# Attention blocks in f32: key tiles in batches of four and five instead of two, with PSUM shared out anew

## The chip, the cores and the metric

The kernel runs on one core of a Trainium2 chip. The core has an engine for matrix products (TensorE, PE in the profile; its weight loads are PEld), one for vectors (VectorE, DVE), one for functions of single elements (ScalarE, ACT), GpSimd (POOL) and SyncE (SP), which here only issues transfers. They run side by side and wait for one another by semaphores. Matrix products are written to PSUM, which has eight banks of 128 partitions x 512 f32; everything else lies in SBUF. The metric is the device time of one execution, in microseconds (us).

## The reference

The input x has 4 images of 128 channels and 96 x 96 pixels, in f32. Two layers of the same form follow each other, each with its own weights:

```
g     = maxpool2(conv1x1(x, g_w, g_b))          # 64 channels, 48 x 48 = 2304 values
theta = conv1x1(x, theta_w, theta_b)            # 64 channels, 9216 queries
phi   = maxpool2(conv1x1(x, phi_w, phi_b))      # 64 channels, 2304 keys
f     = einsum('bqc,bck->bqk', theta, phi)
y     = einsum('bqk,bkc->bqc', softmax(f, axis=-1), g)
W_y   = conv1x1(y, W_w, W_b)                    # back to 128 channels
out   = batchnorm(W_y; gamma, beta, mean, var) + x
```

So each of the 8 blocks (4 images x 2 layers) is an attention of 9216 queries over 2304 keys with 64 channels, and a residual.

## The kernel before

`shifted_blocks` computes all 8 blocks, image by image, layer 0 and then layer 1. The softmax is taken with a constant shift (35) in place of each query's maximum; two running tiles, `rmax` and `rmin`, keep the extremes of the reciprocal sums, and at the very end a flag tells whether any left the safe range. Only then would `general_blocks`, a second version with true maxima, compute everything anew; in the profiled execution none of its lines appears.

A **block** begins with `keys_and_values`: 24 chunks of x go through one product that gives g and phi together (`gphi_ps`, L156), VectorE pools each chunk by a maximum (L159), ScalarE centres phi and copies it to the other 64 partitions (L173, L176), and g is transposed on TensorE (`gT_ps`, L179) and given its bias (L182).

Then come 9 **pairs**. A pair is 2 x 512 queries, `PT` = 1024. Its two halves lie on partitions 0 to 63 and 64 to 127, so that two small products run on TensorE side by side. An f32 product stands as two matmul instructions in the profile, so that what one tile needs is four instructions. There are two shapes:
- `theta` (L200), `values` (L239) and `denominators` (L247) take 128 rows and 64 columns of the array for each half, 128*64 in the profile;
- `scores` (L221) and `project` (L267) take 64 rows and 128 columns, 64*128.

For each of the 18 key tiles (128 keys, `NKT` = 18), `scores(k)` writes a tile of 128 keys x 1024 queries to PSUM (`sc`, two banks), ScalarE takes the exp into SBUF (`exp`, L226, six buffers) and VectorE adds it to a running sum (L230, L232). `values(k)` adds the product of the exp with g to `av` in PSUM, over all 18 tiles. After that, `denominators` sums `sum` over the partitions by a product with ones (`den`), VectorE takes the reciprocals in four pieces (`rc`, L253), multiplies (`y`, L255), and updates `rmax` and `rmin` (L256, L257). `project` multiplies with the output weights (`W_ps`, two tiles of one bank), and VectorE adds the shift and x (L273), in place of x for layer 0 and into a tile that is sent out for layer 1.

The **order** is written by hand at the end of `block` (L286 to L310): key tiles go in batches of `KB` = 2, so nine batches a pair. Step t issues the scores of batch t, then a `project` that has fallen due, then the values of batch t-1, then a `denominators` that has fallen due. The theta of the next pair is issued in the middle of a pair (j = 4). `denominators` follows one step after a pair's last values, `project` three steps after that. What is left at the end of a block is issued at once. On top of this, the framework puts each engine's instructions in order before the run, by its own estimate of what is ready and with program order as priority; each engine then works through its queue in that order.

**PSUM** has eight banks: `ps_sc` 2 tiles of two banks (scores, and the chunks of gphi), `ps_av` 2 of one, `ps_misc` 2 of one (theta, den, W_ps, the transposes). A tile that is asked for while all places of its kind are in use waits until one is released by its last reader.

Of the kernel before, what the change touches and what calls it, by code (L numbers as in the profile page):

```python
# [9 lines left out]
F32 = mybir.dt.float32  # L10
I32 = mybir.dt.int32
AF = mybir.ActivationFunctionType
ALU = mybir.AluOpType
AX = mybir.AxisListType
PSUM = bass.MemoryType.PSUM

P = 128
B, C, CI, H, W = 4, 128, 64, 96, 96
HW = H * W
NK = (H // 2) * (W // 2)  # L20
QT = 512
NQ = HW // QT
KT = 128
NKT = NK // KT
# [7 lines left out]

PT = 2 * QT
NP = HW // PT
KB = 2
NB = NKT // KB
SHIFT = 35.0
SUM_MIN, SUM_MAX = 1e-20, 1e30

# [2 lines left out]
def shifted_blocks(ctx: ExitStack, tc: tile.TileContext, x: bass.AP, layers, out: bass.AP, flag):  # L42
# [11 lines left out]
    nc = tc.nc  # L54
# [3 lines left out]
    xp = ctx.enter_context(tc.tile_pool(name="xp", bufs=2))  # L58
    kvp = ctx.enter_context(tc.tile_pool(name="kvp", bufs=2))
    work = ctx.enter_context(tc.tile_pool(name="work", bufs=2))  # L60
    ps_sc = ctx.enter_context(tc.tile_pool(name="ps_sc", bufs=2, space=PSUM))
    ps_av = ctx.enter_context(tc.tile_pool(name="ps_av", bufs=2, space=PSUM))
    ps_misc = ctx.enter_context(tc.tile_pool(name="ps_misc", bufs=2, space=PSUM))

    ident = const.tile([P, P], F32, name="ident")
    make_identity(nc, ident)
# [6 lines left out]
    rmax = const.tile([P, QT], F32, name="rmax")  # L73
    nc.gpsimd.memset(rmax, 1.0)
    rmin = const.tile([P, QT], F32, name="rmin")
# [132 lines left out]
    class Pair:  # L208
# [9 lines left out]
        def scores(self, k):  # L218
            ps = ps_sc.tile([P, PT], F32, tag="sc", name=f"sc_{self.name}_{k}")
            for h in range(2):  # L220
                nc.tensor.matmul(  # L221
                    ps[:, ts(h, QT)], lhsT=self.phi[ts(h, CI), ts(k, KT)],
                    rhs=self.th[ts(h, CI), :], start=True, stop=True,
                )
            e = work.tile([P, PT], F32, tag="exp", name=f"exp_{self.name}_{k}", bufs=6)
            nc.scalar.activation(e, ps, AF.Exp, bias=nshift)  # L226
            self.es[k] = e
            if k == 1:
                self.sum = work.tile([P, PT], F32, tag="sum", name=f"sum_{self.name}")
                nc.vector.tensor_add(self.sum, self.es[0], e)  # L230
            elif k > 1:
                nc.vector.tensor_add(self.sum, self.sum, e)  # L232

        def values(self, k):
            if k == 0:
                self.av = ps_av.tile([P, QT], F32, tag="av", name=f"av_{self.name}")
            e = self.es.pop(k)
            for h in range(2):
                nc.tensor.matmul(  # L239
                    self.av[ts(h, CI), :], lhsT=self.gT[:, k, :], rhs=e[:, ts(h, QT)],  # L240
                    start=(k == 0), stop=(k == NKT - 1),
                )

        def denominators(self):
            ps = ps_misc.tile([P, QT], F32, tag="misc", name=f"den_{self.name}")
            for h in range(2):
                nc.tensor.matmul(  # L247
                    ps[ts(h, CI), :], lhsT=ones, rhs=self.sum[:, ts(h, QT)],
                    start=True, stop=True,
                )  # L250
            rc = work.tile([P, QT], F32, tag="rc", name=f"rc_{self.name}")
            for i in range(QT // P):
                nc.vector.reciprocal(rc[:, ts(i, P)], ps[:, ts(i, P)])  # L253
            self.y = work.tile([P, QT], F32, tag="y", name=f"y_{self.name}")
            nc.vector.tensor_mul(self.y, self.av, rc)  # L255
            nc.vector.tensor_tensor(rmax, rmax, rc, ALU.max)  # L256
            nc.vector.tensor_tensor(rmin, rmin, rc, ALU.min)  # L257

        def project(self):
            if self.store is not None:  # L260
                dst = work.tile([C, PT], F32, tag="out", name=f"out_{self.name}")
            else:
                dst = self.xt[:, ts(self.p, PT)]
            pss = []
            for h in range(2):
                ps = ps_misc.tile([P, QT], F32, tag="misc", name=f"W_ps_{self.name}_{h}")
                nc.tensor.matmul(  # L267
                    ps, lhsT=self.w["W"][ts(h, CI), :], rhs=self.y[ts(h, CI), :],
                    start=True, stop=True,
                )  # L270
                pss.append(ps)
            for h in range(2):
                nc.vector.scalar_tensor_tensor(  # L273
                    dst[:, ts(h, QT)], pss[h], self.w["shift"],
                    self.xt[:, ts(2 * self.p + h, QT)], op0=ALU.add, op1=ALU.add,
                )
            if self.store is not None:
                nc.sync.dma_start(out=self.store[:, ts(self.p, PT)], in_=dst)

    def block(xt, w, store, name):  # L280
        phi, gT = keys_and_values(xt, w, name)

        def pair(p):
            return Pair(xt, w, phi, gT, p, store, name)

        hooks = {}  # L286
        batches = [(p, j) for p in range(NP) for j in range(NB)]
        pairs = {0: pair(0)}
        for t in range(len(batches) + 1):
            if t < len(batches):  # L290
                p, j = batches[t]
                for k in range(j * KB, (j + 1) * KB):
                    pairs[p].scores(k)
            for step in hooks.pop((t, "rows"), []):
                step()
            if t:
                p, j = batches[t - 1]
                for k in range(j * KB, (j + 1) * KB):
                    pairs[p].values(k)
                if j == NB // 2 and p + 1 < NP:  # L300
                    pairs[p + 1] = pair(p + 1)
                if j == NB - 1:
                    done = pairs.pop(p)
                    hooks.setdefault((t + 1, "columns"), []).append(done.denominators)
                    hooks.setdefault((t + 4, "rows"), []).append(done.project)
            for step in hooks.pop((t, "columns"), []):
                step()
        for key in sorted(hooks):
            for step in hooks[key]:
                step()  # L310

    xt = load_x(0)
    ws = [load_layer(l, p) for l, p in enumerate(layers)]
    for b in range(B):
        nxt = load_x(b + 1) if b + 1 < B else None
        block(xt, ws[0], None, f"{b}_0")
        block(xt, ws[1], out[b].rearrange("c h w -> c (h w)"), f"{b}_1")
        xt = nxt
# [6 lines left out]
    ps = ps_misc.tile([P, QT], F32, tag="misc", name="bad_ps")  # L325
# [7 lines left out]
def general_blocks(ctx: ExitStack, tc: tile.TileContext, x: bass.AP, layers, out: bass.AP):  # L333
# [9 lines left out]
    nc = tc.nc  # L343
# [5 lines left out]
    kvp = ctx.enter_context(tc.tile_pool(name="kvp", bufs=2))  # L349
    work = ctx.enter_context(tc.tile_pool(name="work", bufs=3))  # L350
    ps_max = ctx.enter_context(tc.tile_pool(name="ps_max", bufs=3, space=PSUM))
    ps_sc = ctx.enter_context(tc.tile_pool(name="ps_sc", bufs=2, space=PSUM))
    ps_av = ctx.enter_context(tc.tile_pool(name="ps_av", bufs=2, space=PSUM))
    ps_misc = ctx.enter_context(tc.tile_pool(name="ps_misc", bufs=1, space=PSUM))

    ident = const.tile([P, P], F32, name="ident")
# [240 lines left out]
def nonlocal_blocks(tc: tile.TileContext, x: bass.AP, layers, out: bass.AP):  # L597
    with tc.tile_pool(name="flag", bufs=1) as pool:
        flag = pool.tile([1, 1], I32, name="flag")
        shifted_blocks(tc, x, layers, out, flag)  # L600
        bad = tc.nc.values_load(flag[0:1, 0:1])
        with tc.If(bad > 0):
            general_blocks(tc, x, layers, out)
# [30 lines left out]
```

## Time and profile before

| | |
|---|---|
| time, median of 3 runs (lowest, highest) | 2915.18 us (2915.01, 2915.45) |
| the profiled execution: time, span of its trace | 2915.95 us, 2913.7 us |
| mean granted clock of TensorE | 0.993 |
| exp on ScalarE (L226) | 1296 x 1110 ns |
| sums on VectorE (L232) | 1152 x 1221 ns |
| reciprocals on VectorE (L253) | 288 x 908 ns |
| a score matmul (L221), a value matmul (L239) | 5184 x 615 ns, 5184 x 605 ns |

The profile is of one execution; a row of a timeline gives start, duration, engine, line, operation, output and inputs with shapes and the number of instructions merged into it, and in brackets how long the engine had been idle and what ended that. Matmuls are pipelined and two run side by side here, so their durations overlap and their ends are modelled: what they cost is read from the distance between starts.

### The profile page before, as it was taken

Reading aid. Unit: us, or ns where it says so; the run is one execution under the profiler, and the core shown is the slowest. Engines: PE = TensorE matmul, PEld = TensorE weight load, DVE = VectorE, ACT = ScalarE, POOL = GpSimd, SP = SyncE. Lnnn points to the kernel's source line nnn. Section 1 sums busy time; section 2 is a strip of 40 time slices with the busy share of each in tenths; the row PEclk is TensorE's granted clock in tenths of the full one; section 3 lists DMA queues with packets and bytes.
Section 4 is the critical chain, followed back from the end, with each engine's and each line's share of the span. In section 5 each row is a group of like instructions: output and inputs, shape, how many; then the busy total and the mean of one; then the engine's idle time right before and its main releaser. Section 6 shows DMA issues by size and latency. Waiting matters only on the chain.

```text
span 2913.7 us, 29776 instructions
## 1 busy us (share of the span) xinstructions
PE 2842.7 (98%) x11768; PEld 913.5 (31%) x11768; DVE 2071.7 (71%) x2131; ACT 1467.4 (50%) x1420; POOL 1.6 (0%) x8
## 2 busy tenths in 40 slices
PE   7999999999999999999999999999999999999998
PEld 2333333333333333333333333333333333333332
DVE  4777767777677776777767777677776777767776
ACT  3555535555355553555545555455544555445554
POOL 0000000000000000000000000000000000000000
PEclk9999999999999999999999999999999999999999
DMA  3000000000100000000010000000000000000000
GB/s 135 1 1 1 1 1 15 15 15 15 73 1 1 1 1 0 15 15 15 15 73 1 1 1 0 1 15 15 15 15 8 1 0 1 1 0 15 15 15 23
DMA packets 11604, 40.06 MB, mean 14 GB/s; under 512 B 3393, under 2 KB 3777, under 8 KB 11457
## 3 DMA queue, kind: packets, MB, share of 16 engines
q1 hardware_dynamic: 8640, 37.75, 3.3%
q8 instruction: 94, 1.54, 0.2%
q10 hardware_dynamic: 2816, 0.34, 0.1%
q14 instruction: 54, 0.43, 0.0%
HBM read 19.21 MB, written 18.87 MB: 13 GB/s over the span
## 4 chain that ended last, share of the span: by engine, by line
PE 95%; DVE 2%; ACT 1%; DMA 1%; issue 0%; ACTq 0%
PE sc L221 42%; PE av L239 41%; PE gphi_ps L156 4%; PE theta_ps L200 2%; PE W_ps L267 2%; PE den L247 2%; DVE rc L253 1%; DVE gphi L159 1%; PE gT_ps L179 1%; DMA theta_b<-in_L_conv_theta_b_dram 0%; ACT exp L226 0%; DVE centre L169 0%; ACT phi L173 0%; DMA W_nat<-in_L_conv_W_w_dram 0%; ACT phi L176 0%; DMA theta_nat<-in_L_conv_theta_w_dram 0%
## 5 line engine op out<-in xcount | busy, mean ns | idle before, releaser
L226 ACT ACTIVATE exp<-sc,nshift 128x1024 f32<-128x1024 f32 x1296 | 1372.5, 1110 | 1083.7 <-PE sc L221 1083.5
L232 DVE TENSOR_TENSOR sum<-sum,exp 128x1024 f32<-128x1024 f32 x1152 | 1406.3, 1221 | 556.6 <-ACT exp L226 492.2
L221 PE MATMUL sc<-theta,phi 64*128 64x512 f32 x5184 | 1289.0, 615 | 12.6 <-ACT exp L226 8.0
L239 PE MATMUL av<-exp,gT 128*64 128x512 f32 x5184 | 1253.5, 605 | 0.0
L221 PEld LDWEIGHTS sc<-theta,phi 64*128 64x128 f32 x5184 | 445.3, 186 | 840.3 <-issue 457.3
L239 PEld LDWEIGHTS av<-exp,gT 128*64 128x64 f32 x5184 | 315.0, 136 | 859.8 <-issue 853.7
L253 DVE RECIPROCAL rc<-den 128x128 f32<-128x128 f32 x288 | 243.7, 908 | 12.8 <-PE den L247 12.8
L230 DVE TENSOR_TENSOR sum<-exp,exp 128x1024 f32<-128x1024 f32 x72 | 88.2, 1225 | 175.7 <-ACT exp L226 175.7
L156 PE MATMUL gphi_ps<-x,gphiT 128*128 128x384 f32 x384 | 170.5, 556 | 35.6 <-DVE gphi L159 30.5
L159 DVE TENSOR_REDUCE gphi<-gphi_ps 128x96 f32<-128x384 f32 x192 | 105.5, 554 | 62.7 <-PE gphi_ps L156 57.5
L205 ACT ACTIVATE theta<-theta_ps,theta_b 128x512 f32<-128x512 f32 x72 | 49.5, 687 | 150.1 <-PE theta_ps L200 150.1
L173 ACT ACTIVATE phi<-gphi,centre 64x768 f32<-64x768 f32 x24 | 22.3, 930 | 172.1 <-DVE centre L170 136.1
L156 PEld LDWEIGHTS gphi_ps<-x,gphiT 128*128 128x128 f32 x384 | 66.4, 202 | 101.3 <-DVE gphi L159 56.3
L200 PE MATMUL theta_ps<-x,thetaT 128*64 128x512 f32 x288 | 84.0, 595 | 0.0
L267 PE MATMUL W_ps<-y,WT 64*128 64x512 f32 x288 | 77.2, 614 | 4.2 <-DVE y L255 4.2
L247 PE MATMUL den<-sum,ones 128*64 128x512 f32 x288 | 74.0, 592 | 0.0
L273 DVE SCALAR_TENSOR_TENSOR x<-W_ps,shift,x 128x512 f32<-128x512 f32 x72 | 53.6, 744 | 2.7 <-PE W_ps L267 2.7
L273 DVE SCALAR_TENSOR_TENSOR out<-W_ps,shift,x 128x512 f32<-128x512 f32 x72 | 53.5, 744 | 0.8 <-PE W_ps L267 0.8
L257 DVE TENSOR_TENSOR rmin<-rmin,rc 128x512 f32<-128x512 f32 x72 | 49.3, 684 | 0.0
L256 DVE TENSOR_TENSOR rmax<-rmax,rc 128x512 f32<-128x512 f32 x72 | 49.0, 681 | 0.0
L255 DVE TENSOR_TENSOR y<-av,rc 128x512 f32<-128x512 f32 x72 | 48.7, 677 | 0.0
L267 PEld LDWEIGHTS W_ps<-y,WT 64*128 64x128 f32 x288 | 27.4, 188 | 39.1 <-issue 15.8
(45 smaller groups left out, 144.2 us busy)
## 6 DMA issues: line engine op xcount, KB each, us to landing
x<-in_x_dram SPq DMA_DIRECT2D x24, 768.0 KB, 7.5
out_dram<-out SPq DMA_DIRECT2D x36, 512.0 KB, 2.6
theta_nat<-in_L_conv_theta_w_dram ACTq DMA_DIRECT2D x2, 32.0 KB, 5.4
theta_b<-in_L_conv_theta_b_dram ACTq DMA_DIRECT2D x4, 0.2 KB, 6.1
gphi_nat<-in_L_conv_g_w_dram ACTq DMA_DIRECT2D x2, 32.0 KB, 5.6
gphi_nat<-in_L_conv_phi_w_dram ACTq DMA_DIRECT2D x2, 32.0 KB, 5.2
g_b<-in_L_conv_g_b_dram ACTq DMA_DIRECT2D x2, 32.0 KB, 5.5
W_nat<-in_L_conv_W_w_dram ACTq DMA_DIRECT2D x2, 32.0 KB, 5.9
```

The lines of the kernel that those rows point to most:

```text
L156: nc.tensor.matmul(ps[:, :CC], lhsT=w["gphi"], rhs=xt[:, ts(r, CC)], start=True, stop=True)
L159: nc.vector.tensor_reduce(gphi[:, ts(r, CC // 4)].rearrange("p (h w) -> p h w", w=W // 2), ps[:, :CC].rearrange("p (h a w b) -> p h w a b" ...
L200: nc.tensor.matmul(ps[ts(h, CI), :], lhsT=w["theta"], rhs=xt[:, ts(2 * p + h, QT)], start=True, stop=True,)
L221: nc.tensor.matmul(ps[:, ts(h, QT)], lhsT=self.phi[ts(h, CI), ts(k, KT)], rhs=self.th[ts(h, CI), :], start=True, stop=True,)
L226: nc.scalar.activation(e, ps, AF.Exp, bias=nshift)
L230: nc.vector.tensor_add(self.sum, self.es[0], e)
L232: nc.vector.tensor_add(self.sum, self.sum, e)
L239: nc.tensor.matmul(self.av[ts(h, CI), :], lhsT=self.gT[:, k, :], rhs=e[:, ts(h, QT)], start=(k == 0), stop=(k == NKT - 1),)
L247: nc.tensor.matmul(ps[ts(h, CI), :], lhsT=ones, rhs=self.sum[:, ts(h, QT)], start=True, stop=True,)
L253: nc.vector.reciprocal(rc[:, ts(i, P)], ps[:, ts(i, P)])
L267: nc.tensor.matmul(ps, lhsT=self.w["W"][ts(h, CI), :], rhs=self.y[ts(h, CI), :], start=True, stop=True,)
L273: nc.vector.scalar_tensor_tensor(dst[:, ts(h, QT)], pss[h], self.w["shift"], self.xt[:, ts(2 * self.p + h, QT)], op0=ALU.add, op1=ALU.add,)
```

## The change

The key tiles of a pair go in four batches of 4, 5, 4 and 5 in place of nine of 2. `ps_sc` gets a third tile (six banks), `ps_av` and `ps_misc` keep one bank each; there are ten exp buffers in place of six.

`denominators` is issued one step earlier, ahead of the pair's last values, and ends with the reciprocals. Behind the last values, ScalarE copies `av` to SBUF, and VectorE multiplies that copy with the reciprocals and updates `rmax` and `rmin`. `project` comes one step later, behind the scores of the next pair's second batch, into one tile of the scores' kind (two banks), and one addition of 128x1024 takes the place of two of 128x512. The next pair's theta is issued behind the values of the second batch. The pools of `general_blocks` are shared out anew as well.

```diff
-KB = 2
-NB = NKT // KB
+BATCHES = ((0, 1, 2, 3), (4, 5, 6, 7, 8), (9, 10, 11, 12), (13, 14, 15, 16, 17))
+NB = len(BATCHES)
...
-    ps_sc = ctx.enter_context(tc.tile_pool(name="ps_sc", bufs=2, space=PSUM))
-    ps_av = ctx.enter_context(tc.tile_pool(name="ps_av", bufs=2, space=PSUM))
-    ps_misc = ctx.enter_context(tc.tile_pool(name="ps_misc", bufs=2, space=PSUM))
+    ps_sc = ctx.enter_context(tc.tile_pool(name="ps_sc", bufs=3, space=PSUM))
+    ps_av = ctx.enter_context(tc.tile_pool(name="ps_av", bufs=1, space=PSUM))
+    ps_misc = ctx.enter_context(tc.tile_pool(name="ps_misc", bufs=1, space=PSUM))
...
-            e = work.tile([P, PT], F32, tag="exp", name=f"exp_{self.name}_{k}", bufs=6)
+            e = work.tile([P, PT], F32, tag="exp", name=f"exp_{self.name}_{k}", bufs=10)
...
+            if k == NKT - 1:
+                self.y = work.tile([P, QT], F32, tag="y", name=f"y_{self.name}")
+                nc.scalar.copy(self.y, self.av)
+                nc.vector.tensor_mul(self.y, self.y, self.rc)
+                nc.vector.tensor_tensor(rmax, rmax, self.rc, ALU.max)
+                nc.vector.tensor_tensor(rmin, rmin, self.rc, ALU.min)
...
-            rc = work.tile([P, QT], F32, tag="rc", name=f"rc_{self.name}")
+            self.rc = rc = work.tile([P, QT], F32, tag="rc", name=f"rc_{self.name}")
             for i in range(QT // P):
                 nc.vector.reciprocal(rc[:, ts(i, P)], ps[:, ts(i, P)])
-            self.y = work.tile([P, QT], F32, tag="y", name=f"y_{self.name}")
-            nc.vector.tensor_mul(self.y, self.av, rc)
-            nc.vector.tensor_tensor(rmax, rmax, rc, ALU.max)
-            nc.vector.tensor_tensor(rmin, rmin, rc, ALU.min)
...
-            pss = []
+            ps = ps_sc.tile([P, PT], F32, tag="sc", name=f"W_ps_{self.name}")
             for h in range(2):
-                ps = ps_misc.tile([P, QT], F32, tag="misc", name=f"W_ps_{self.name}_{h}")
                 nc.tensor.matmul(
-                    ps, lhsT=self.w["W"][ts(h, CI), :], rhs=self.y[ts(h, CI), :],
-                    start=True, stop=True,
-                )
-                pss.append(ps)
-            for h in range(2):
-                nc.vector.scalar_tensor_tensor(
-                    dst[:, ts(h, QT)], pss[h], self.w["shift"],
-                    self.xt[:, ts(2 * self.p + h, QT)], op0=ALU.add, op1=ALU.add,
-                )
+                    ps[:, ts(h, QT)], lhsT=self.w["W"][ts(h, CI), :],
+                    rhs=self.y[ts(h, CI), :], start=True, stop=True,
+                )
+            nc.vector.scalar_tensor_tensor(
+                dst, ps, self.w["shift"], self.xt[:, ts(self.p, PT)],
+                op0=ALU.add, op1=ALU.add,
+            )
...
-        for t in range(len(batches) + 1):
+        ending = None
+        for t in range(len(batches) + 2):
             if t < len(batches):
                 p, j = batches[t]
-                for k in range(j * KB, (j + 1) * KB):
+                for k in BATCHES[j]:
                     pairs[p].scores(k)
-            for step in hooks.pop((t, "rows"), []):
-                step()
-            if t:
+            if ending is not None:
+                ending.project()
+                ending = None
+            if 0 < t <= len(batches):
                 p, j = batches[t - 1]
-                for k in range(j * KB, (j + 1) * KB):
+                if j == NB - 1:
+                    ending = pairs[p]
+                    ending.denominators()
+                for k in BATCHES[j]:
                     pairs[p].values(k)
-                if j == NB // 2 and p + 1 < NP:
+                if j == 1 and p + 1 < NP:
                     pairs[p + 1] = pair(p + 1)
-                if j == NB - 1:
-                    done = pairs.pop(p)
-                    hooks.setdefault((t + 1, "columns"), []).append(done.denominators)
-                    hooks.setdefault((t + 4, "rows"), []).append(done.project)
-            for step in hooks.pop((t, "columns"), []):
-                step()
-        for key in sorted(hooks):
-            for step in hooks[key]:
-                step()
```

More of the change, by code (lines that the diff above doesn't have):

```diff
@@ L284, in pair @@
             return Pair(xt, w, phi, gT, p, store, name)
-        hooks = {}
         batches = [(p, j) for p in range(NP) for j in range(NB)]
         pairs = {0: pair(0)}
-        for t in range(len(batches) + 1):
+        ending = None
+        for t in range(len(batches) + 2):
             if t < len(batches):
                 p, j = batches[t]
-                for k in range(j * KB, (j + 1) * KB):
+                for k in BATCHES[j]:
                     pairs[p].scores(k)
-            for step in hooks.pop((t, "rows"), []):
-                step()
-            if t:
+            if ending is not None:
+                ending.project()
+                ending = None
+            if 0 < t <= len(batches):
                 p, j = batches[t - 1]
-                for k in range(j * KB, (j + 1) * KB):
+                if j == NB - 1:
+                    ending = pairs[p]
+                    ending.denominators()
+                for k in BATCHES[j]:
                     pairs[p].values(k)
-                if j == NB // 2 and p + 1 < NP:
+                if j == 1 and p + 1 < NP:
                     pairs[p + 1] = pair(p + 1)
-                if j == NB - 1:
-                    done = pairs.pop(p)
-                    hooks.setdefault((t + 1, "columns"), []).append(done.denominators)
-                    hooks.setdefault((t + 4, "rows"), []).append(done.project)
-            for step in hooks.pop((t, "columns"), []):
-                step()
-        for key in sorted(hooks):
-            for step in hooks[key]:
-                step()
     xt = load_x(0)
@@ L351, in general_blocks @@
     ps_max = ctx.enter_context(tc.tile_pool(name="ps_max", bufs=3, space=PSUM))
-    ps_sc = ctx.enter_context(tc.tile_pool(name="ps_sc", bufs=2, space=PSUM))
-    ps_av = ctx.enter_context(tc.tile_pool(name="ps_av", bufs=2, space=PSUM))
+    ps_sc = ctx.enter_context(tc.tile_pool(name="ps_sc", bufs=3, space=PSUM))
+    ps_av = ctx.enter_context(tc.tile_pool(name="ps_av", bufs=1, space=PSUM))
     ps_misc = ctx.enter_context(tc.tile_pool(name="ps_misc", bufs=1, space=PSUM))
```

## The prediction

> **What bounds the kernel.** I read the page's busy line first, then the chain, then the timeline of TensorE.
>
> ```profile
> PE 2842.7 (98%) x11768; PEld 913.5 (31%) x11768; DVE 2071.7 (71%) x2131; ACT 1467.4 (50%) x1420; POOL 1.6 (0%) x8
> ...
> PE 95%; DVE 2%; ACT 1%; DMA 1%; issue 0%; ACTq 0%
> ...
> 1026.78:1063.41 36.63, 36.63 (x158) 11.51 (x156) 26.91 (x27) 19.75 (x19) 0.00 (x0) 1.00 0.00 0
> ```
>
> TensorE is busy for 98% and is 95% of the chain. The third line is one pair (1024 queries) from the view by windows: 36.63 us, TensorE busy throughout at granted clock 1.00, VectorE for 26.9, ScalarE for 19.75. So only less time on TensorE makes this faster, and the timeline says what its time goes to (start, duration, line, count):
>
> ```profile
> 1002.35 1.99 PE L221 MATMUL sc<-theta,phi 64*128 64x512 f32 x8
> 1004.17 1.02 PE L267 MATMUL W_ps<-y,WT 64*128 64x512 f32 x4
> 1005.12 1.94 PE L239 MATMUL av<-exp,gT 128*64 128x512 f32 x8
> 1006.99 1.99 PE L221 MATMUL sc<-theta,phi 64*128 64x512 f32 x8
> 1008.91 1.94 PE L239 MATMUL av<-exp,gT 128*64 128x512 f32 x8
> 1010.68 1.03 PE L200 MATMUL theta_ps<-x,thetaT 128*64 128x512 f32 x4
> 1011.63 1.99 PE L221 MATMUL sc<-theta,phi 64*128 64x512 f32 x8
> 1013.55 1.94 PE L239 MATMUL av<-exp,gT 128*64 128x512 f32 x8
> 1015.42 1.99 PE L221 MATMUL sc<-theta,phi 64*128 64x512 f32 x8
> ...
> 373.47 3.65 PE L239 MATMUL av<-exp,gT 128*64 128x512 f32 x16
> 376.95 1.03 PE L247 MATMUL den<-sum,ones 128*64 128x512 f32 x4
> 377.91 1.56 PE L156 MATMUL gphi_ps<-x,gphiT 128*128 128x384 f32 x4
> 381.89 0.91 PE L156 MATMUL gphi_ps<-x,gphiT 128*128 128x384 f32 x2 [2.42 <-DVE gphi L159]
> ```
>
> Read starts, not durations. Eight score matmuls (two key tiles) take 1.92 from start to start when values follow (1006.99 to 1008.91), but 1.82 when W_ps follows (1002.35 to 1004.17), which has the same shape, 64*128. Eight value matmuls take 1.86 before scores (1013.55 to 1015.42), 1.77 before theta_ps, also 128*64. And sixteen value matmuls in one stretch take 3.48, so eight more cost 1.71. One more tile therefore costs 0.855, and theta or W_ps too: 1.77 + 0.95 + 1.92 (theta included) less 3.79 (without) is 0.85. A step of two score and two value tiles takes 1.92 + 1.87 = 3.79, its work 4 x 0.855 = 3.42. What remains, **0.37 us, is two changes of shape**, 0.18 each. The pair checks: 39 units of 0.855 (18 + 18 tiles, theta, den, W) plus 9 x 0.37 is 36.7 against 36.63.
>
> The Trainium skill, "TensorEngine Tiling (Array Packing)", Key Properties, says that changing the tiling mode drains TensorE, though not what it costs; by that rule the saving below follows, and the trace agrees with 0.18 us a change.
>
> **Batches of 4, 5, 4, 5.** Nine alternations of a pair become four; den goes ahead of values, theta stays behind values and W_ps behind scores, so none adds a change. 10 changes fewer x 0.183 x 72 pairs = **-131 us**, if nothing interrupts a batch. A pair is then 33.35 + 4 x 0.37 = 34.83. Bounds: the 3.48 stretch shows the price for value batches of 4; for score batches the nearest row is scores plus W_ps (12 matmuls in 2.77). I see no reason for a loss inside a batch except the next item.
>
> **Three score tiles, longer bursts.** Now ScalarE and VectorE must keep up within a batch.
>
> ```profile
> L226 ACT ACTIVATE exp<-sc,nshift 128x1024 f32<-128x1024 f32 x1296 | 1372.5, 1110 | 1083.7 <-PE sc L221 1083.5
> 1008.17 2.12 ACT L226 ACTIVATE exp<-sc,nshift 128x1024 f32<-128x1024 f32 x2 [2.52 <-PE sc L221]
> ...
> 410.12 1.99 PE L221 MATMUL sc<-theta,phi 64*128 64x512 f32 x8 [0.57 <-ACT theta L205]
> 413.07 2.13 PE L221 MATMUL sc<-theta,phi 64*128 64x512 f32 x8 [0.97 <-ACT exp L226]
> 415.14 1.94 PE L239 MATMUL av<-exp,gT 128*64 128x512 f32 x8
> ...
> 411.91 2.12 ACT L226 ACTIVATE exp<-sc,nshift 128x1024 f32<-128x1024 f32 x2
> ```
>
> The first exp starts 1.18 after its batch (1008.17 - 1006.99), takes 1.11, and the next starts 1.01 later (2.12 - 1.11). So exps of a batch end at 2.29, 3.30, 4.31, 5.32, 6.33, while score tiles start at 0, 0.96, 1.82, 2.68, 3.53. With two tiles the third would wait; at 413.07 it does, 0.05 after the exp that ended at 413.02, and that stretch runs 0.15 longer (2.07) since its weights weren't loaded ahead. With three tiles the fourth (2.68) needs the exp of 2.29, the fifth (3.53) that of 3.30: no wait. W_ps, now a score tile behind a batch of five, wants 4.39 and gets 4.36: at most 0.1 for weights loaded late, x 64 = +6 (0 to 10).
>
> **The W_ps tile gives its place back late.** It is read by one addition of 128x1024 on VectorE, and the next batch's third tile takes its place if places come free in turn. VectorE's queue:
>
> ```profile
> 1029.10 2.55 DVE L232 TENSOR_TENSOR sum<-sum,exp 128x1024 f32<-128x1024 f32 x2 [1.55 <-ACT exp L226]
> 1031.57 3.39 DVE L253 RECIPROCAL rc<-den 128x128 f32<-128x128 f32 x4
> 1034.87 1.16 DVE L232 TENSOR_TENSOR sum<-sum,exp 128x1024 f32<-128x1024 f32 x1
> 1035.95 0.68 DVE L255 TENSOR_TENSOR y<-av,rc 128x512 f32<-128x512 f32 x1
> 1036.54 0.68 DVE L256 TENSOR_TENSOR rmax<-rmax,rc 128x512 f32<-128x512 f32 x1
> 1037.14 0.68 DVE L257 TENSOR_TENSOR rmin<-rmin,rc 128x512 f32<-128x512 f32 x1
> 1037.74 2.55 DVE L232 TENSOR_TENSOR sum<-sum,exp 128x1024 f32<-128x1024 f32 x2
> ...
> 2906.11 1.41 DVE L273 SCALAR_TENSOR_TENSOR out<-W_ps,shift,x 128x512 f32<-128x512 f32 x2
> ```
>
> A sum takes 1.33 from start to start (2.55 - 1.22), four reciprocals 3.30, y, rmax, rmin 0.6 each. Call 0 the start of the next pair's first batch. TensorE: 4 scores to 3.63; den and 5 values to 8.92; 5 scores to 13.31, W_ps to 14.26; 4 values to 17.84; then batch three, its third tile due at 19.66, with W_ps's delay about 19.75. VectorE in program order: three sums from 3.3, reciprocals 7.1 to 10.4, y at 10.5, rmax, rmin, from 12.3 five sums, at 18.75 the addition. For 128x1024 no row: a sum of that size takes 1.22, two halves back to back 1.41; I take 1.3, between them. It ends at 20.05, so the tile gets its place at 20.1: 0.4 late, and 0.1 for its weights. **0.5 x 64 = +32 us** (72 pairs less the last of each block). Bounds: 0 if the addition is queued ahead of the last sum (then 18.75 in place of 20.05); 1.0 a pair, +64, if the chain is half a microsecond slower.
>
> **The copy of av on ScalarE** (72). No row; theta's activation of a 128x512 PSUM tile is nearest:
>
> ```profile
> L205 ACT ACTIVATE theta<-theta_ps,theta_b 128x512 f32<-128x512 f32 x72 | 49.5, 687 | 150.1 <-PE theta_ps L200 150.1
> ```
>
> 0.69 lies at 9.05 to 9.75, before the exp of 10.1 and with y held by the reciprocals until 10.5: nothing. Without that cover it is 0.69 x 72 = 50 in the exps behind it; below nothing it can't go. av's single bank is free at 9.75, the next values come at 14.26. y then reads SBUF; a gain or loss there goes into the 0.5 above. theta and den share one small bank: den's is free when the reciprocals end (10.4), theta comes at 22. Ten exp buffers cover the nine tiles alive.
>
> **Block ends.** Before, den, reciprocals and y stand in a row before W_ps, and TensorE loses 2.42 + 1.39 (before 381.89 and 385.86) in seven blocks, 4.22 in the last:
>
> ```profile
> 385.86 1.62 PE L156 MATMUL gphi_ps<-x,gphiT 128*128 128x384 f32 x2 [1.39 <-DVE gphi L159]
> ...
> 2903.67 2.08 PE L267 MATMUL W_ps<-y,WT 64*128 64x512 f32 x4 [4.22 <-DVE y L255]
> ...
> 406.16 1.07 PE L200 MATMUL theta_ps<-x,thetaT 128*64 128x512 f32 x2
> ...
> 409.58 0.56 DVE L182 TENSOR_TENSOR gT<-gT_ps,g_b 128x384 f32<-128x384 f32 x1 [0.91 <-PE gT_ps L179]
> ```
>
> After, the reciprocals lie beside five values (4.3 us); but den comes 4 values after the last scores, at 8.1 of that batch, and five sums end at 8.9: 0.9 lost, and about 1.3 around y. Gain 1.5 a block, **-12** (0 to -30). At the start theta must wait for the one small bank until gT is added (409.58 + 0.56), where half of it now runs at 406.16: 0.7 a block, **+6** (0 to +12). Nine scores in a row wait for exps about as long as four did. The transposes of the weights behind one bank, and the general version's pools (none of its lines has a row): nothing.
>
> **Sum**: -131 + 6 + 32 - 12 + 6 = -99. The profiled execution took 2915.95 (span 2913.7, 2.25 around it), the median of the runs is 2915.18: **2816** from the median, 0.8 more from the profiled one.
>
> **Rivals.** (a) The third tile doesn't wait, because the addition stands one sum earlier in VectorE's queue. For it: before, L273's halves stand on either side of a sum; against: the whole addition needs both halves, later than the last exp's sum is ready. 2816 - 32 = 2784.
> (b) **ScalarE sets the pace, slower than before**: if in effect only two score tiles rotate, a tile starts when the exp two before it has ended: the fifth at 4.35 in place of 3.53, the fourth at 3.35 in place of 2.68, each with 0.1 for weights: 2 x 0.9 + 2 x 0.8 = 3.4 a pair. Above 1.83 a pair the change loses; here it is 2915 + 72 x 1.6 = 3030. Against it: 3 tiles are asked for; for it: exps come at 1.01, tiles at 0.855.
> The same page of the Trainium skill, Performance Considerations (PSUM Bottleneck), says that tiling speeds up TensorE but not the emptying of PSUM, which may become the bound; by that rule (b) holds within a batch, and no run here shows a third score tile.
> (c) The W_ps tile's place is next in turn for the first tile, not the third: 20.1 - 17.9 = 2.2 a pair in place of 0.5, 2816 + 109 = 2925.
> (d) It doesn't do what it says: the framework orders instructions itself and tears each pair's batches once: two changes more, 0.37 x 72 = 26: 2842.
>
> **Chances.** Forecast 0.60, (a) 0.17, (d) 0.08, (b) 0.06, (c) 0.05, within 0.2% (about 6 us, what a measurement can tell from no change) 0.04. Faster 0.87: forecast, (a), (d) and a little of (c). The range 2770 to 2858 takes (a) with the largest gain at block ends below, and above a wait of 1.0 (+32) with no gain at block ends; it leaves out (b) and (c).
>
> **What would show it.** Right: TensorE's timeline alternates 16 and 20 matmuls, scores of 16 in about 3.6 and values of 16 in 3.6; a pair lasts 35.3 to 35.5; an idle place of about 0.4 before the third tile of batch three, released by L273's successor on VectorE. Wrong: waits of scores for exp inside batches (b), for VectorE at the first tile (c), stretches of other counts (d), or a change of shape that costs more behind long stretches than 0.18.

## The result and the profile after

The changed kernel takes **2760.78 us** (median of 4 runs, 2758.19 to 2761.31) against 2915.28 before (4 runs, 2915.01 to 2915.45): a ratio of 0.947, 95% interval 0.945 to 0.949. That is 154.5 us less, where 99 less were forecast, and 9 us below the lower end of the range. The profiled execution has a span of 2759.0 us at a mean granted clock of 0.996.

The page's busy line and chain, and from the view by windows one pair:

```profile
PE 2697.5 (98%) x11768; PEld 962.5 (35%) x11768; DVE 2079.8 (75%) x2059; ACT 1475.4 (53%) x1492; POOL 1.6 (0%) x8
...
PE 91%; DVE 5%; ACT 2%; issue 1%; DMA 1%; ACTq 0%; DVEq 0%
...
895.01:930.24 35.23, 35.20 (x158) 12.21 (x156) 27.02 (x26) 19.87 (x20) 0.00 (x0) 1.00 0.00 1
```

TensorE still sets the time, and still has 11768 matmuls. A pair takes 35.23 us in place of 36.63, at the same granted clock; VectorE and ScalarE do as much in it as before. 1.40 x 72 pairs is 101 us. So some 54 of the 154.5 were won outside the pairs, where one block ends and the next starts, and the forecast had put 6 there.

TensorE's timeline over the same pair:

```profile
895.01 3.70 PE L221 MATMUL sc<-theta,phi 64*128 64x512 f32 x16
898.64 1.08 PE L253 MATMUL den<-sum,ones 128*64 128x512 f32 x4
899.55 4.46 PE L239 MATMUL av<-exp,gT 128*64 128x512 f32 x20
903.94 4.56 PE L221 MATMUL sc<-theta,phi 64*128 64x512 f32 x20
908.34 1.09 PE L268 MATMUL W_ps<-y,WT 64*128 64x512 f32 x4
909.36 3.65 PE L239 MATMUL av<-exp,gT 128*64 128x512 f32 x16
912.94 4.00 PE L221 MATMUL sc<-theta,phi 64*128 64x512 f32 x16
916.87 4.51 PE L239 MATMUL av<-exp,gT 128*64 128x512 f32 x20
921.21 1.03 PE L200 MATMUL theta_ps<-x,thetaT 128*64 128x512 f32 x4
922.17 4.56 PE L221 MATMUL sc<-theta,phi 64*128 64x512 f32 x20
926.66 3.65 PE L239 MATMUL av<-exp,gT 128*64 128x512 f32 x16
930.25 1.99 PE L221 MATMUL sc<-theta,phi 64*128 64x512 f32 x8
```

The batches stand whole, in the order of the code (the last row is cut off by the end of the window). Sixteen scores ahead of den take 3.63 from start to start (895.01 to 898.64), which was forecast to the hundredth; the sixteen that follow W_ps and four value tiles take 3.93 (912.94 to 916.87). W_ps takes 1.02 where it took 0.95.

What TensorE waits for there, in the view of waits (total, times, longest), and VectorE's timeline before it:

```profile
PEld sc L221 <- DVE out L272: 28.0, 32, 1.2
PEld sc L221 <- DVE x L272: 27.7, 32, 1.2
```

```profile
905.35 0.69 DVE L247 TENSOR_TENSOR rmax<-rmax,rc 128x512 f32<-128x512 f32 x1
905.96 0.69 DVE L246 TENSOR_TENSOR y<-y,rc 128x512 f32<-128x512 f32 x1
906.57 0.69 DVE L248 TENSOR_TENSOR rmin<-rmin,rc 128x512 f32<-128x512 f32 x1
907.17 6.54 DVE L232 TENSOR_TENSOR sum<-sum,exp 128x1024 f32<-128x1024 f32 x5
913.62 1.28 DVE L272 SCALAR_TENSOR_TENSOR x<-W_ps,shift,x 128x1024 f32<-128x1024 f32 x1
```

64 waits for the addition that reads W_ps, as many as pairs that are not the last of a block. (The time in these rows is that in which no weight load ran, not TensorE's loss, which is 0.30.) The addition starts at 18.61 of the pair (913.62 - 895.01) and ends at 19.89; 18.75 and 20.05 were worked out. In the trace the second score tile of that stretch starts at 913.90 and the third at 914.95, 0.05 behind the end of the addition (914.90). That is 0.19 later than in the stretch ahead of den, where the third starts 0.86 after the second, and the third tile itself then takes 0.97 in place of 0.86: together the 0.30.

The end of a block and the start of the next, on TensorE:

```profile
1031.53 3.65 PE L239 MATMUL av<-exp,gT 128*64 128x512 f32 x16
1035.95 1.08 PE L253 MATMUL den<-sum,ones 128*64 128x512 f32 x4 [0.77 <-DVE sum L232]
1036.86 4.46 PE L239 MATMUL av<-exp,gT 128*64 128x512 f32 x20
1042.83 1.13 PE L268 MATMUL W_ps<-y,WT 64*128 64x512 f32 x4 [1.50 <-DVE y L246]
1043.89 6.23 PE L156 MATMUL gphi_ps<-x,gphiT 128*128 128x384 f32 x18
1050.05 0.58 PE L179 MATMUL gT_ps<-ident,gphi 64*128 64x64 f32 x6
1050.56 2.20 PE L156 MATMUL gphi_ps<-x,gphiT 128*128 128x384 f32 x6
...
1063.22 1.08 PE L200 MATMUL theta_ps<-x,thetaT 128*64 128x512 f32 x4 [0.65 <-DVE gT L182]
1065.09 9.90 PE L221 MATMUL sc<-theta,phi 64*128 64x512 f32 x36 [0.79 <-ACT theta L205]
```

The losses of 0.77 at den and 1.50 at y are about those forecast (0.9 and 1.3). But from the first gphi chunk to the first scores it is 21.20 us, where before it was 32.21 (377.91 to 410.12; every second block 29.72). The two don't hold the same: before, W_ps and the waits of 2.42 and 1.39 lie behind the first chunk, now W_ps and the wait for y lie ahead of it. Counted alike, from den to the first scores, with den's wait and without the five value tiles that now stand in between (4.39), it is 25.5 where it was 33.2 (376.95 to 410.12) or, every second block, 30.7. Part of what went away shows in the rows of before:

```profile
397.05 0.33 PE L179 MATMUL gT_ps<-ident,gphi 64*128 64x64 f32 x2
397.32 1.56 PE L156 MATMUL gphi_ps<-x,gphiT 128*128 128x384 f32 x4
398.81 0.27 PE L179 MATMUL gT_ps<-ident,gphi 64*128 64x64 f32 x1
399.01 0.91 PE L156 MATMUL gphi_ps<-x,gphiT 128*128 128x384 f32 x2
399.85 0.27 PE L179 MATMUL gT_ps<-ident,gphi 64*128 64x64 f32 x1
```

Before, the transposes of g stood one or two at a time among the chunks, in 93 stretches over the whole kernel: two shapes again, 128*128 and 64*128, with a change each way. A chunk's two matmuls cost 0.84 there (399.01 to 399.85); in the stretch of eighteen after the change they cost 0.68 (6.16 / 9). Now the six transposes of a third of the keys stand together, and there are 25 stretches. No line of the diff says so: the framework orders them. What made it do so was the open question.

### The profile page after: what moved, and what is told of

It is laid out like the page before. It is cut to its first block, busy times and chain, and to the rows that moved or that the text cites. A ratio compares the mean times of both kernels' runs of the same rounds, so it can differ in the third digit from the quotient of the medians.

```text
span 2759.0 us, 29743 instructions
## 1 busy us (share of the span) xinstructions
PE 2697.5 (98%) x11768; PEld 962.5 (35%) x11768; DVE 2079.8 (75%) x2059; ACT 1475.4 (53%) x1492; POOL 1.6 (0%) x8
## 4 chain that ended last, share of the span: by engine, by line
PE 91%; DVE 5%; ACT 2%; issue 1%; DMA 1%; ACTq 0%; DVEq 0%
PE sc L221 41%; PE av L239 39%; PE gphi_ps L156 4%; PE den L253 3%; PE W_ps L268 2%; PE theta_ps L200 2%; DVE sum L232 2%; ACT exp L226 1%; DVE gphi L159 1%; DVE rc L259 0%; DVE gT L182 0%; DVE y L246 0%; DVE centre L169 0%; PE gT_ps L179 0%; DMA var<-in_L_conv_bn_var_dram 0%
## 5 line engine op out<-in xcount | busy, mean ns | idle before, releaser
L226 ACT ACTIVATE exp<-sc,nshift 128x1024 f32<-128x1024 f32 x1296 | 1338.3, 1117 | 562.0 <-PE sc L221 561.8
L221 PE MATMUL sc<-theta,phi 64*128 64x512 f32 x5184 | 1216.9, 607 | 9.1 <-ACT theta L205 6.3
L239 PE MATMUL av<-exp,gT 128*64 128x512 f32 x5184 | 1172.2, 596 | 0.0
L221 PEld LDWEIGHTS sc<-theta,phi 64*128 64x128 f32 x5184 | 471.6, 187 | 750.3 <-issue 482.3
L239 PEld LDWEIGHTS av<-exp,gT 128*64 128x64 f32 x5184 | 353.0, 137 | 780.5 <-issue 780.5
L245 ACT COPY y<-av 128x512 f32<-128x512 f32 x72 | 42.2, 586 | 304.1 <-PE av L239 304.1
L156 PE MATMUL gphi_ps<-x,gphiT 128*128 128x384 f32 x384 | 136.1, 501 | 4.1 <-DVE gphi L159 3.6
L268 PE MATMUL W_ps<-y,WT 64*128 64x512 f32 x288 | 78.6, 622 | 12.4 <-DVE y L246 12.4
L200 PE MATMUL theta_ps<-x,thetaT 128*64 128x512 f32 x288 | 74.4, 595 | 5.2 <-DVE gT L182 5.2
L246 DVE TENSOR_TENSOR y<-y,rc 128x512 f32<-128x512 f32 x72 | 49.3, 685 | 1.3 <-ACT y L245 1.3
L272 DVE SCALAR_TENSOR_TENSOR x<-W_ps,shift,x 128x1024 f32<-128x1024 f32 x36 | 46.0, 1279 | 5.3 <-PE W_ps L268 5.3
L272 DVE SCALAR_TENSOR_TENSOR out<-W_ps,shift,x 128x1024 f32<-128x1024 f32 x36 | 46.0, 1279 | 4.4 <-PE W_ps L268 4.4
```

The source lines that it names most:

```text
L156: nc.tensor.matmul(ps[:, :CC], lhsT=w["gphi"], rhs=xt[:, ts(r, CC)], start=True, stop=True)
L200: nc.tensor.matmul(ps[ts(h, CI), :], lhsT=w["theta"], rhs=xt[:, ts(2 * p + h, QT)], start=True, stop=True,)
L221: nc.tensor.matmul(ps[:, ts(h, QT)], lhsT=self.phi[ts(h, CI), ts(k, KT)], rhs=self.th[ts(h, CI), :], start=True, stop=True,)
L239: nc.tensor.matmul(self.av[ts(h, CI), :], lhsT=self.gT[:, k, :], rhs=e[:, ts(h, QT)], start=(k == 0), stop=(k == NKT - 1),)
L268: nc.tensor.matmul(ps[:, ts(h, QT)], lhsT=self.w["W"][ts(h, CI), :], rhs=self.y[ts(h, CI), :], start=True, stop=True,)
L272: nc.vector.scalar_tensor_tensor(dst, ps, self.w["shift"], self.xt[:, ts(self.p, PT)], op0=ALU.add, op1=ALU.add,)
```

## The experiments

**1. The third place alone.** The chunks of gphi use the score tiles' places, of which there are three now.

```diff
 # the kernel before
+            if r % 3 == 2:
+                ps = ps_av.tile([P, QT], F32, tag="av", name=f"gphi_ps_{name}_{r}")
+            else:
+                ps = ps_sc.tile([P, PT], F32, tag="sc", name=f"gphi_ps_{name}_{r}")
```

> The kernel before, with one thing of the change alone: every third gphi chunk gets its PSUM tile from the av pool, so that three chunks can be in flight in place of two; batches of two key tiles, den, project and all else as before. Theory 1 (the third place lets TensorE run on through the chunks, so that the transposes of g stay in stretches of six and the waits of gphi for VectorE go): the stretch from the first gphi chunk to the first scores falls from 32.2 us to 22 to 26 us per block, in all -50 to -80 us against 2915. Rival 2 (the block start got shorter because the reciprocals no longer stand ahead of the pooling in VectorE's queue): they still stand there, so the stretch stays at 30 to 32 us, in all 0 to -15 us. Rival 3 (the single small bank made the transposes come in stretches): two banks remain, so no change, 0 us.

2871.90 us, ratio 0.986 (0.984 to 0.988): 42 less than the 2913.6 of the runs beside it. From first chunk to first scores it is 26.4 in place of 32.2 or 29.7. Both miss the ranges of theory 1 by a little, and are far more than rivals 2 and 3 allow. But its mechanism came true only in part: the transposes stand in 70 stretches, fewer than 93, and not in stretches of six, and gphi still waits for VectorE.

**2. The third place held.**

```diff
 # the changed kernel
+        held = ps_sc.tile([P, PT], F32, tag="sc", name=f"held_{name}")
+        nc.tensor.matmul(held[:, :CC], lhsT=w["gphi"], rhs=xt[:, ts(0, CC)], start=True, stop=True)
         for r in range(HW // CC):
...
+        spare = work.tile([P, CC // 4], F32, tag="spare", name=f"spare_{name}")
+        nc.vector.tensor_tensor(spare, held[:, : CC // 4], gphi[:, ts(HW // CC - 1, CC // 4)], ALU.max)
```

> The changed kernel, with one of its three score tiles held occupied from the first to the last gphi chunk of each block (one more chunk product per block, 0.7 us, and one small operation of VectorE that releases it); otherwise as changed. Theory 1: the transposes are strewn among the chunks again and the stretch from first gphi to first scores rises from 21.2 us to 27 to 32 us per block, in all +45 to +85 us against 2761. Rivals 2 and 3: only the work added counts, +6 to +12 us.

2795.37 us, ratio 0.960 (0.958 to 0.961): 35 more than the changed kernel, of which 0.75 x 8 = 6 is the added product. The stretch from the first chunk behind it to the first scores is 25.36, so 4.16 a block more than 21.20, some 32 us in all (the first block gives 3.3). That lies between the two expectations and nearer to theory 1, whose mechanism is there: the transposes are strewn again, in 92 stretches.

```profile
1062.71 0.27 PE L179 MATMUL gT_ps<-ident,gphi 64*128 64x64 f32 x1
1062.91 0.91 PE L156 MATMUL gphi_ps<-x,gphiT 128*128 128x384 f32 x2
```

The groups by line show where the time lies, first the kernel before, then experiment 1, experiment 2 and the changed kernel (count | busy, mean ns | idle before):

```profile
L156 PE MATMUL gphi_ps<-x,gphiT 128*128 128x384 f32 x384 | 170.5, 556 | 35.6 <-DVE gphi L159 30.5 <-DVE gphiT L98 4.5
...
L179 PE MATMUL gT_ps<-ident,gphi 64*128 64x64 f32 x144 | 29.0, 259 | 0.0
...
L200 PE MATMUL theta_ps<-x,thetaT 128*64 128x512 f32 x288 | 84.0, 595 | 0.0
```

```profile
L159 PE MATMUL gphi_ps<-x,gphiT 128*128 128x384 f32 x384 | 149.3, 516 | 21.8 <-DVE gphi L162 16.7 <-DVE gphiT L98 5.0
...
L182 PE MATMUL gT_ps<-ident,gphi 64*128 64x64 f32 x144 | 23.6, 246 | 0.0
```

```profile
L156 PE MATMUL gphi_ps<-x,gphiT 128*128 128x384 f32 x384 | 160.4, 528 | 4.8 <-DVE gphi L159 4.3
...
L179 PE MATMUL gT_ps<-ident,gphi 64*128 64x64 f32 x144 | 30.0, 258 | 3.1 <-DVE gphi L159 3.1
```

```profile
L156 PE MATMUL gphi_ps<-x,gphiT 128*128 128x384 f32 x384 | 136.1, 501 | 4.1 <-DVE gphi L159 3.6 <-DVE gphiT L98 0.4
...
L179 PE MATMUL gT_ps<-ident,gphi 64*128 64x64 f32 x144 | 15.9, 234 | 2.0 <-DVE gphi L159 1.6 <-DVE centre L170 0.5
...
L200 PE MATMUL theta_ps<-x,thetaT 128*64 128x512 f32 x288 | 74.4, 595 | 5.2 <-DVE gT L182 5.2
```

Between the last two kernels the third place differs (and the small work that holds it): with it free, gphi falls by 24.3 busy and gT by 14.1, while the waits stay small in both. The two together are more than the 32 us read from starts, since the modelled durations overlap where the lines alternate. So within the changed kernel the place works by TensorE's order, hardly by shorter waits. How much of that is the change of shape can be worked out from the rows of before: a second chunk in a row costs 0.65 (1.49 for two, 397.32 to 398.81, less 0.84), so 0.19 of a lone chunk's 0.84 goes with the change; six transposes take 0.51 (1050.05 to 1050.56) and one takes 0.20 (399.85 to 400.05), so 0.14 of that does. An alternation is then some 0.33 here, near the 0.37 of the pairs, and 67 of them fewer are an estimated 22 of the 32 us. What makes up the rest isn't shown.

The waits, 35.6 before, fell to 21.8 in experiment 1, where the place came alone and the reciprocals still stood ahead of the chunks in VectorE's queue, and are at 4.8 in experiment 2, where the reciprocals have moved and the place is held. So up to 31 us of these waits went with the rest of the change, most likely with the reciprocals' move (rival 2), and some 14 of them the place alone would also take; they can't be added up. New waits stand against them, at den (6.5) and at W_ps (12.4 where it was 4.2).

Theta's two halves, which were strewn too, stand in one piece now (84.0 busy to 74.4, with 5.2 of waiting). That is not the third place's doing: they stand in one piece where it is held, and are strewn in experiment 5, which has two small banks again. Rival 3 is out for the transposes: with one small bank and the place held they are strewn. Why the framework strews the transposes with two places for the chunks, and hardly with three, would follow if it keeps to program order but lets what is ready go ahead of what must wait for a place; its estimates were not looked into, so this is argued and not shown.

**3. Twice the alternations.**

```diff
 # the changed kernel; in each step t
-                for k in BATCHES[j]:
+                for k in BATCHES[j][:2]:
                     pairs[p].scores(k)
...
-                for k in BATCHES[j]:
+                for k in BATCHES[j][:2]:
                     pairs[p].values(k)
...
 # and behind these: scores of [2:], the project that is due, values of [2:]
```

> The changed kernel with each batch of four or five issued as two halves (two scores, two values, the remaining scores, the remaining values), so that scores and values alternate eight times a pair in place of four; buffers, den, project and theta as changed. If a change of shape costs 0.18 us wherever it stands: 8 more a pair, +1.46 us, x 72 = +105 us, less up to 21 us where the 0.30 us wait of the third score tile for VectorE goes: +84 to +105. If instead the gain of the pairs came from the changed places of den, project and the buffers: +0 to +30 us.

2836.23 us, ratio 0.974 (0.971 to 0.976): 75 more than the changed kernel, 9 below the lower end of the expected range. One pair, from W_ps to W_ps:

```profile
901.22 1.02 PE L268 MATMUL W_ps<-y,WT 64*128 64x512 f32 x4
...
937.51 1.02 PE L268 MATMUL W_ps<-y,WT 64*128 64x512 f32 x4
```

36.29, so 1.06 more than 35.23. Four alternations at 0.366 are 1.46; the wait behind W_ps (0.30) and W_ps's own delay (0.07, not subtracted in the expectation) go, which makes 1.09. So the price of an alternation holds, worked out in this way after the run, and the rival, at most 30 us, falls.

**4. What the third tile behind W_ps waits for.** First by program order alone:

```diff
 # the changed kernel; out of values(), into project() behind the addition
+            nc.vector.tensor_tensor(rmax, rmax, self.rc, ALU.max)
+            nc.vector.tensor_tensor(rmin, rmin, self.rc, ALU.min)
```

> The changed kernel with the updates of rmax and rmin moved from ahead of the next five sums to behind the addition that reads W_ps, so that this addition starts 1.2 us earlier in VectorE's queue. Theory (the third score tile of the second batch behind W_ps waits for this addition): its score stretch falls from 3.93 to 3.63 us, 0.30 x 64 = -19 us. Rival (the 0.30 us is the price of three tiles behind a batch of five, whatever VectorE does): 0 us.

2759.82 us, ratio 0.948 (0.946 to 0.950), no change. But VectorE's timeline shows that nothing was tried: the framework puts both where they were, presumably because VectorE was free there by its estimate.

```profile
903.64 0.69 DVE L274 TENSOR_TENSOR rmax<-rmax,rc 128x512 f32<-128x512 f32 x1
904.25 0.69 DVE L246 TENSOR_TENSOR y<-y,rc 128x512 f32<-128x512 f32 x1
904.85 0.69 DVE L275 TENSOR_TENSOR rmin<-rmin,rc 128x512 f32<-128x512 f32 x1
```

So once more with a dependency that holds them back:

```diff
 # the changed kernel; in place of those two, in project() behind the addition
+            zero = work.tile([P, 1], F32, tag="zero", name=f"zero_{self.name}")
+            nc.vector.tensor_scalar(zero, dst[:, :1], 0.0, None, ALU.mult)
+            nc.vector.scalar_tensor_tensor(rmax, self.rc, zero, rmax, op0=ALU.add, op1=ALU.max)
+            nc.vector.scalar_tensor_tensor(rmin, self.rc, zero, rmin, op0=ALU.add, op1=ALU.min)
```

> The changed kernel with the updates of rmax and rmin tied behind the addition that reads W_ps (each takes a zero that is worked out from that addition's result, one more small operation of VectorE a pair), so that they can't be put ahead of it. Theory (the third score tile of the batch behind W_ps waits for this addition, which comes 1.2 us earlier now): that score stretch falls from 3.93 to 3.63 us, -0.30 x 64 = -19 us against 2761. Rival (0.30 us is the price of three tiles behind a batch of five, whatever VectorE does): 0 us.

2746.19 us, ratio 0.943 (0.941 to 0.945), some 12 to 15 less than the changed kernel. TensorE behind W_ps:

```profile
909.89 3.70 PE L221 MATMUL sc<-theta,phi 64*128 64x512 f32 x16
913.53 4.51 PE L239 MATMUL av<-exp,gT 128*64 128x512 f32 x20
```

The stretch takes 3.64 in place of 3.93: the whole wait is gone, so the addition's place in VectorE's queue was its cause. Of the 19 us some 7 are given back at block starts, where the stretch from chunks to scores is 22.04 in place of 21.20 (0.84 x 8); the transposes stand in 32 stretches there.

**5. Two score tiles**, the rival (b) of the prediction as a run (`ps_sc` 2, `ps_av` 2, `ps_misc` 2).

> The changed kernel with two score tiles in place of three (and two banks each for the small ones), all else as changed. By the working of the prediction's rival (b): a tile starts when the exp two before it has ended, 3.4 us more a pair than without waits, so about 38.2 us a pair, and the transposes at block starts are strewn again (+35 us in all): 2970 to 3030 us. If the order of the exps didn't hold TensorE: 2761 plus those 35, about 2795 us.

3064.42 us, ratio 1.052 (1.050 to 1.054): slower than before, and by 34 us more than the upper end.

```profile
918.50 1.99 PE L221 MATMUL sc<-theta,phi 64*128 64x512 f32 x8
920.84 2.13 PE L221 MATMUL sc<-theta,phi 64*128 64x512 f32 x8 [0.36 <-ACT exp L226]
922.91 1.08 PE L253 MATMUL den<-sum,ones 128*64 128x512 f32 x4
```

A batch of four takes 4.41 (918.50 to 922.91) where three tiles give 3.63: 0.78, as worked out. A batch of five takes 5.74 (909.17 to 914.91 in the trace) where three tiles give 4.49, so 1.25 and not the 0.9 of the working: a pair takes 39.08 and not 38.2, which accounts for the miss. Batches of four and five need the third tile to be worth anything.

**6. Batches of six.**

```diff
 # the changed kernel
-BATCHES = ((0, 1, 2, 3), (4, 5, 6, 7, 8), (9, 10, 11, 12), (13, 14, 15, 16, 17))
+BATCHES = ((0, 1, 2, 3, 4, 5), (6, 7, 8, 9, 10, 11), (12, 13, 14, 15, 16, 17))
-            e = work.tile([P, PT], F32, tag="exp", name=f"exp_{self.name}_{k}", bufs=10)
+            e = work.tile([P, PT], F32, tag="exp", name=f"exp_{self.name}_{k}", bufs=13)
-                if j == 1 and p + 1 < NP:
+                if j == 0 and p + 1 < NP:
```

> The changed kernel with three batches of six key tiles a pair (13 exp buffers; theta of the next pair behind the first batch's values). Theory (0.37 us for each alternation, and three score tiles still suffice: sixth tile wanted at 4.39 us of its batch, place free at 4.36): a pair is 33.35 + 3 x 0.37 = 34.46 plus about 0.3 for weights loaded late, against 35.23 now; with the den's wait at block ends gone (-7) and some 4 us more of waiting in the first scores of a block, 2715 to 2745 us. Rival (the exps set the pace beyond five tiles): the sixth tiles wait and a pair stays at 35.2 or rises; 2755 to 2800 us.

2723.96 us, ratio 0.936 (0.934 to 0.938), inside the first range. The same batch of two pairs in a row (the second row is cut off by the end of the window):

```profile
896.38 5.48 PE L221 MATMUL sc<-theta,phi 64*128 64x512 f32 x24
...
931.25 1.13 PE L221 MATMUL sc<-theta,phi 64*128 64x512 f32 x4
```

A pair is 34.87 (34.46 plus 0.3 were expected). TensorE stands idle for no exp within these batches, but its weight loads for scores wait for exps for 327.3 us in all, where it was 169.8 in the changed kernel: six tiles are about what three places bear.

**7. A fourth place for the chunks** (every fourth chunk in the bank of `av`).

> The changed kernel with a fourth place for gphi chunks (every fourth chunk in the bank of av, which no pair needs then). If the places of the chunks still hold TensorE at block starts: the stretch from first gphi to first scores falls below 21.2 us by what its waits for VectorE amount to, at most 0.4 us per block, in all 0 to -4 us against 2761. If three places are what it takes: 0 us, no change.

2751.79 us, ratio 0.945 (0.943 to 0.946), the changed kernel 0.947 (0.945 to 0.949): 6 to 9 less, but the intervals overlap. Neither expectation says where the gain would come from. The transposes stand as they did, in 25 stretches, and the stretch from the first chunk to the first scores doesn't fall, it is 21.87, since it holds W_ps now: a chunk runs ahead of W_ps, where TensorE waited 1.50 for y, so that the waits of W_ps fall from 12.4 to 1.8 in all, while gphi waits 4.8 for the copy of av instead.

**8. Six and the fourth place together**, and the changed kernel once more on the same chip.

> Batches of six and the fourth place for gphi chunks together. If the two gains lie in different stretches (pairs, block starts) they add: about 2724 less 8, 2712 to 2720 us. If the fourth place only moved a wait that the batches of six have already taken (the den's at block ends): 2722 to 2726 us.

> The changed kernel once more, unaltered, on the chip of the run before it: 2758 to 2762 us.

2718.70 us, ratio 0.934 (0.932 to 0.935), and 2757.87 us, ratio 0.947 (0.945 to 0.948). The first lies in the range that adds the two gains and is the fastest version found, 39 us below the changed kernel beside it; from batches of six alone it can't be told apart with certainty (5 us, the intervals overlap).

## Why the prediction was wrong

The direction was right, and so was the mechanism in the pairs; the size was off by 55 us, and 48 of them lie in one step, the block ends and starts, where a mechanism was overlooked.

- **What bounds the kernel**: right. TensorE sets the time, and an alternation of shapes costs 0.37 us. Experiment 3 doubled the alternations and paid 1.06 a pair, where 1.09 follows from that price once the waits that went are taken off. The Trainium skill's rule ("TensorEngine Tiling (Array Packing)", Key Properties: a change of tiling mode drains TensorE) agrees with it; the price is this case's.
- **Batches of 4, 5, 4, 5**: -131 us for the pairs less 38 of waits, so -93; measured 1.40 x 72 = 101. A pair was to take 35.43 with its waits and takes 35.23.
- **Three score tiles** within a batch: right. No score waits for an exp inside a batch; W_ps is 0.07 late, "at most 0.1". Two tiles in the changed kernel give 3064 (experiment 5), above rival (b)'s 3030.
- **The W_ps tile gives its place back late**: the mechanism is right to its place (experiment 4), mis-sized: 0.30 a pair where 0.5 was put, so 19 us and not 32. The addition ended 0.16 earlier than worked out, which is most of the difference. Rival (a), no wait, and (c), the first tile in place of the third, are out.
- **The copy of av**: hidden as said; it takes 586 ns (L245), against the 0.69 taken from theta's row.
- **Block ends, -12, and starts, +6**: this is the step that failed; -6 was forecast and some -54 measured. It asked only which of the known waits would go and come, and took TensorE's order between them as given. For the waits it was about right: those of gphi, gT, den and W_ps come to 39.8 before and to 26.7 in experiment 2, 13 less, some 4 of them at the start of the kernel. But the third place, put into the sum only within the score batches, also serves the chunks of gphi, and there it changed the order: with the place held the transposes stand in 92 stretches, with it free in 25, and that is some 32 us (4.16 a block, experiment 2). Put alone into the kernel before, the place took 38 us from the eight block starts, 14 of them waits, with 70 stretches for 93 (experiment 1). The forecast had priced a change of shape in the pairs and not looked for the same alternation at block starts, where its own quoted row showed one half of theta standing alone (406.16). Theta adds about 10 us to the miss: it waits 0.65 a block, as forecast (0.7), but its halves run in one piece now, so that its rows gain 4.4 where +6 was put. The few us left were not taken apart.
- **Rival (d)**, that the framework tears the batches: out in the pairs. That it reorders was seen, but only as a danger.
- **The Trainium skill's rule on PSUM emptying** (same page, Performance Considerations, PSUM Bottleneck) came true with two score tiles (ratio 1.052), where TensorE stands idle for exps for 138.5 us. With three it did not: TensorE is 91% of the chain in the changed kernel and 97% with batches of six.

## What to carry to other kernels

Price a change of shape on TensorE from the distances between starts, and then count the changes in every stage, not in the one that the edit names: here a third of the gain came from the passage from block to block, and a fifth of it (32 us) from code that the diff leaves as it was. When a pool gets another buffer, list every user of that pool, and ask for each whether an engine that used to fill a wait with other work will now run straight on. To move an operation in a queue that a framework orders, give it a dependency; its place in the program may do nothing (experiment 4).

## What the runs showed of the hardware

The price of a change of shape did not grow with the stretches around it: 0.37 us for an alternation, read from batches of two, gives the pair with batches of four and five (33.35 + 4 x 0.37, 0.30 for the wait and 0.07 for W_ps, 35.20 against 35.23). With batches of six a pair lies 0.41 above 33.35 + 3 x 0.37; late weights can be the reason, so that this run doesn't show the price by itself. And small products strewn among large ones cost more than their own time: a chunk's two matmuls cost 0.84 us between single transposes and 0.68 in a long stretch, a transpose alone costs 0.20 and six together cost 0.51.
